# First block of rows ahead of the other rows and the router; search rounds placed behind the scan, with their counts on PE

## The chip, the core and the metric

One Trainium2 chip, and on it one core. The metric is the device time of the kernel in microseconds (us). Five engines with queues of their own work side by side: PE (matrix products; its weight loads are listed as PEld), DVE (vector), ACT (activation functions), POOL (the second vector engine, which also issues indirect transfers) and SP (which issues the other transfers). An instruction waits at the head of its engine's queue until what it needs is done, and all behind it waits too.

## What is computed

Two layers over x, 8 sequences of 256 rows of 128 numbers. Each layer adds an attention-like part and a mixture of experts to its input. The change lies in the first layer alone:

```python
xn = _layernorm(x)
x = x + ssm(xn, ...) + ffn(xn, ...)          # first layer
# ssm: a layer norm of xn, with ln_g and ln_b, then
#   X_main = silu(conv(Xn @ W_up1));  pp = X_main @ W_ll + b_ll
#   delta = softplus(pp[..., :D]);  Bm, Cm = the rest of pp
#   A = -exp(A_log)                           # D = 256 channels, N = 16 states
#   H = exp(delta * A) * H + U;  y = sum_n C * H    (256 steps for each sequence)
#   out = (y * silu(Xn @ W_up2)) @ W_down + b_down
# ffn: scores = softmax(xn @ Wr)              # 2048 rows, 8 experts
#   G, idx = top_k(scores.T, 512)             # each expert takes its 512 best rows
#   out[idx] += G * expert(xn[idx])
```

## The kernel before

**Order of the work.** Inside the first layer the order of PE, ACT, DVE and POOL is the program's own order (`manual_schedule`, L152): what is written first is first in the engine's queue. Generators that `yield` are advanced by hand from the main loop, so the place of a `next(...)` decides where a piece of work stands in every queue.

**Ahead of the scan.** x is loaded in four quarters (L187), then A_log and the weights, all from SP's queue. DVE takes mean and variance of 16 chunks of 128 rows (`bn_stats`, `bn_aggr`, L229 to L234), with A = -exp(A_log) and its reciprocal between them (L231, L232). From these, for all chunks at once, come the scales `rs`, `rv`, `nm` (two square roots on ACT, L235 and L248). POOL builds `dg` (L239: four instructions) and then `wcv`, the weights of W_up1 times the convolution (L242). ACT scales each chunk to `xh` (L279: both layer norms in one), DVE to `xn` (L255); PE transposes both (L272), and ACT and DVE copy the results to `XnT` and `xnT` (L287, L292), quarter by quarter. PE then computes the router's logits `pl` (L736: 16 products with 8 columns), and a softmax follows on DVE and ACT. `xn` and the softmax are written to `xn_d`, from which the experts' rows are gathered.

**`front(q)`** (L303) prepares block q, two sequences of 512 rows: four products `pu` with `wcv` (L314) and a SiLU each (L318), the gate `pg` (L327), delta from `pd` (L353, with softplus by L357 to L375), B and C from `pbc` (L364), and transposes `pxT` (L393), whose halves are swapped by four transfers to `xS` (L402). It yields ten times. Block 0 is prepared ahead of the scan, blocks 1 to 3 inside it (from k = 0, 17 and 33).

**The scan** is a loop over 64 units k (L781; 8 sequences, 4 groups of states, 2 halves of the channels). In each: DVE does `u = (ab - 1) * u` (L688) and the scan (L692); PE does `x_times_b(k + 1)` (u, L670) and `sums(k - 2)` (py, L705); POOL multiplies h by C (L696) and spreads B (L654); ACT computes the decays for k + 2 (L680). u has two PSUM buffers, ab three, h four.

**The search** (L427) finds each expert's threshold, three bits a round, in ten rounds: DVE makes 7 candidates (L429), compares all scores with them (`ge`, L433) and adds up each partition's 16 hits (`cp`, L439); then the generator yields; then PE adds over the partitions (`pc`, L442), and DVE keeps the bits (L447 to L451). Three more pieces find the chosen rows and their slots. Six pieces are advanced by `front(0)`'s yields, the others at the end of the units k = 0 to 7, behind front's piece. The end of the search sets `SEL0` (8 here): from there one expert's rows are selected every 5 units (`select`, L518), and seven units later the experts begin (`experts`, L582; five units each). The rows that they add to, `acc_d`, are first filled with x + xn + bdown by POOL (`base`, L765, one addition in each of the units 0 to 7).

PSUM tiles called `bank(...)` come from one pool with two buffers (`ps_m`), so each waits until the last but one has been read.

Of the kernel before, what the change touches and what calls it, by code (L numbers as in the profile page):

```python
# [8 lines left out]
F32 = mybir.dt.float32  # L9
I32 = mybir.dt.int32  # L10
BF16 = mybir.dt.bfloat16
# [31 lines left out]
SB = 3  # L43
BK = 64
# [6 lines left out]
def block_kernel(ctx: ExitStack, tc: tile.TileContext, a: dict, out: bass.AP):  # L51
# [98 lines left out]
    with ExitStack() as l0:  # L150
# [13 lines left out]

        def exp_and_ln():

            nc.scalar.add_instruction(
                mybir.InstLoadActFuncSet(
                    name=nc.get_next_instruction_name(), act_func_set_id=EXP_LN, ins=[], outs=[]
                )  # L170
            )
# [11 lines left out]

        x = main.tile([P, NC, DM], F32, name="x", tag="c8")
# [3 lines left out]
        alog = load0("alog", [P, ND, N], a["alog"].rearrange("(c p) n -> p c n", p=P))  # L188
# [7 lines left out]
        ln_b = load0("ln_b", [P, 1])  # L196
        wr0 = load0("wr0", [P, E0])
        conv_b = load0("conv_b", [P, ND])
# [6 lines left out]
        wup2 = load0("wup2", [P, D])  # L205
        wll = load0("wll", [P, ND, D + 2 * N], a["wll"].rearrange("(c p) e -> p c e", p=P))
        bll_d = load0("bll_d", [P, ND])
        bll_bc = load0("bll_bc", [2 * N, 1])
# [15 lines left out]
        sd = main.tile([P, NC], F32, name="sd")  # L224
        exp_and_ln()
# [3 lines left out]
        for c in range(NC):  # L229
            if c == 8:  # L230
                nc.vector.tensor_scalar(An, An, -1.0, None, ALU.mult)  # L231
                nc.vector.reciprocal(rA, An)  # L232
            nc.vector.bn_stats(st[:, c, :], x[:, c, :])
            nc.vector.bn_aggr(mv[:, c, :], st[:, c, :])  # L234
        nc.scalar.activation(sd, mv[:, :, 1], AF.Sqrt, bias=eps_t)  # L235

        for dc in range(ND):
            for n in range(0, N, 8):
                nc.gpsimd.tensor_tensor(  # L239
                    dg[:, dc, n : n + 8], bc(eye, 1, 8), bc(rA[:, dc, n : n + 8], 2, BK), ALU.mult  # L240
                )
        nc.gpsimd.tensor_tensor(wcv, bc(wup1, 1, K), conv_w, ALU.mult)  # L242
        rs = main.tile([P, NC], F32, name="rs")
        nc.vector.reciprocal(rs, sd)
        vi = main.tile([P, NC], F32, name="vi")
        nc.vector.tensor_mul(vi, mv[:, :, 1], rs)
        nc.vector.tensor_mul(vi, vi, rs)
        nc.scalar.activation(vi, vi, AF.Sqrt, bias=eps_t)  # L248
        nm = main.tile([P, NC], F32, name="nm")
        nc.vector.scalar_tensor_tensor(nm, mv[:, :, 0], -1.0, rs, ALU.mult, ALU.mult)  # L250
        xn = main.tile([P, NC, DM], F32, name="xn", tag="d8")
        xh = main.tile([P, NC, DM], F32, name="xh", tag="a8")

        def normalize(c):
            nc.vector.tensor_scalar(  # L255
                xn[:, c, :], x[:, c, :], mv[:, c, 0:1], rs[:, c : c + 1], ALU.subtract, ALU.mult
            )

        normalize(0)
        nc.vector.reciprocal(vi, vi)  # L260
        rv = main.tile([P, NC], F32, name="rv")
        nc.vector.tensor_mul(rv, rs, vi)
        nc.vector.tensor_mul(nm, nm, vi)
        xnT = main.tile([P, NT], F32, name="xnT", tag="b8")

        pts = {}

        def transposes(h, lo, src, nm_):
            if lo == 0:
                pts[h, nm_] = ps_u.tile([P, 8, P], F32, name=f"pt_{nm_}{h}", tag="u")  # L270
            for j in range(lo, lo + 4):
                nc.tensor.transpose(pts[h, nm_][:, j, :], src[:, 8 * h + j, :], ident)  # L272

        for h in range(2):
            for g in range(2):
                q = 2 * h + g
                cols = slice(q * BLK, (q + 1) * BLK)
                for c in range(4 * q, 4 * q + 4):
                    nc.scalar.activation(  # L279
                        xh[:, c, :], x[:, c, :], AF.Identity,  # L280
                        bias=nm[:, c : c + 1], scale=rv[:, c : c + 1],
                    )
                    if c:
                        normalize(c)
                transposes(h, 4 * g, xh, "xh")
                transposes(h, 4 * g, xn, "xn")
                nc.scalar.activation(  # L287
                    XnT[:, 2 * q : 2 * q + 2, K - 1 :],
                    pts[h, "xh"][:, 4 * g : 4 * g + 4, :].rearrange("p (b j) l -> p b (j l)", j=2),
                    AF.Identity, bias=ln_b, scale=ln_g,  # L290
                )
                nc.vector.tensor_copy(  # L292
                    xnT[:, cols], pts[h, "xn"][:, 4 * g : 4 * g + 4, :].rearrange("p j l -> p (j l)")
                )
        xn_dv = xn_d.rearrange("(p c) d -> p c d", p=P)
        nc.sync.dma_start(xn_dv[:, :, 0:DM], xn)
# [130 lines left out]
        def search():  # L427
            for i in range(30 // SB):
                nc.vector.tensor_tensor(  # L429
                    cand, bc(thr, 1, NK), bc(bits[:, i, :], 2, E0), ALU.bitwise_or  # L430
                )
                ge = main.tile([P, NK, E0, NC], BF16, name=f"ge{i}", tag="ge")
                nc.vector.tensor_tensor(  # L433
                    ge, bc(sc, 1, NK), bc(cand.bitcast(F32), 3, NC), ALU.is_ge
                )

                cp = main.tile([P, NK, E0], BF16, name=f"cp{i}", tag="cp", bufs=2)
                with nc.allow_low_precision(reason="whole numbers up to 16"):
                    nc.vector.tensor_reduce(cp, ge, AX.X, ALU.add)  # L439
                yield  # L440
                pc = bank(f"pc{i}", [P, NK, E0])
                nc.tensor.matmul(  # L442
                    pc.rearrange("p k e -> p (k e)"), ones_b, cp.rearrange("p k e -> p (k e)"),
                    start=True, stop=True,
                )
                keep = main.tile([P, NK, E0], I32, name=f"keep{i}", tag="keep", bufs=2)
                nc.vector.tensor_scalar(keep, pc, CAP - 0.5, None, ALU.is_ge)  # L447
                m = main.tile([P, E0], I32, name=f"m{i}", tag="m", bufs=2)
                with nc.allow_low_precision(reason="whole numbers up to 7"):
                    nc.vector.tensor_reduce(m, keep.rearrange("p k e -> p e k"), AX.X, ALU.add)  # L450
                nc.vector.scalar_tensor_tensor(  # L451
                    thr, m, 30 - SB * (i + 1), thr, ALU.logical_shift_left, ALU.bitwise_or
                )
# [113 lines left out]
        def scatter(e, s, oc):  # L567
# [6 lines left out]
            if s:  # L574
                tc.declare_no_dep(
                    i.ins, group=f"added{e}", reason="an expert's rows are all different"
                )
            after_all(i, acc0, added[4 * (e - 1) : 4 * e] if e else [])
# [155 lines left out]
        pl = bank("pl", [P, NC, E0])  # L734
        for c in range(NC):
            nc.tensor.matmul(  # L736
                pl[:, c, :], xnT[:, c * P : (c + 1) * P], wr0, start=True, stop=True
            )
        mx = main.tile([P, NC], F32, name="mx")
        nc.vector.tensor_reduce(mx, pl, AX.X, ALU.max)  # L740
        ex = main.tile([P, NC, E0], F32, name="ex")
        nc.vector.tensor_tensor(ex, pl, bc(mx, 2, E0), ALU.subtract)
        exp_and_ln()
        nc.scalar.activation(ex, ex, AF.Exp)
        sm = main.tile([P, NC], F32, name="sm")
        nc.vector.tensor_reduce(sm, ex, AX.X, ALU.add)
        nc.vector.reciprocal(sm, sm)
        nc.vector.tensor_mul(ex, ex, bc(sm, 2, E0))
        nc.sync.dma_start(xn_dv[:, :, DM:], ex)
        nc.vector.tensor_copy(sc, ex.rearrange("p c e -> p e c"))  # L750
        nc.vector.memset(thr, 0)
        find = search()
        next(find)
        for i, _ in enumerate(front(0)):
            if i % 2 and i < 10:
                next(find)
# [6 lines left out]


        def base():  # L765
            for h in range(4):
                t = x[:, 4 * h : 4 * h + 4, :]
                nc.gpsimd.tensor_add(t, t, xn[:, 4 * h : 4 * h + 4, :])
                yield
                nc.gpsimd.tensor_add(t, t, bc(bdown, 1, 4))  # L770
                yield
            acc0.append(nc.sync.dma_start(acc_d.rearrange("(p c) d -> p c d", p=P), x))

        acc0 = []
        running = [find, base()]
        START = {0: [front, 1], 17: [front, 2], 33: [front, 3]}
# [4 lines left out]
        for k in range(len(units) + 4):  # L781
            if k in START:
                f, q = START[k]
                running.insert(0, f(q))
# [5 lines left out]
            part = next(work, None) if 0 in XgT else None  # L790
# [21 lines left out]
            for t in list(running):  # L812
                if next(t, 0) == 0:
                    running.remove(t)
                    if t is find:
                        SEL0 = k + 1
# [609 lines left out]
```

## Time and profile before

| what | us |
|---|---|
| median of 3 runs (lowest, highest) | 701.22 (697.59, 703.15) |
| profiled execution | 702.32 |
| its span, from first to last instruction | 700.4 |
| first transpose on PE | 18.0 |
| first product of block 0 | 35.5 |
| first scan instruction of unit 0 | 68.0 |
| first scan instruction of unit 63 | 431.4 |
| busy: PE, DVE, POOL, ACT | 560.8, 428.2, 381.8, 332.5 |

The profile lists one execution. A line of the timeline has start, duration (both in us), engine, line of the kernel, operation, output and inputs, shapes and the number of instructions merged into it; behind it in brackets the idle time of the engine just before, and what ended that. A line of the stages has the stretch, its length, busy time (and instructions) of PE, PEld, DVE, ACT and POOL, the granted clock of PE, the busy share of the DMA engines and their GB/s.

### The profile page before, as it was taken

The page shows a single profiled execution, that of the slowest core. Times are in us where ns is not written, and L with a number is a line of the kernel's source. Part 1 is how long each engine was busy: PE and PEld are TensorE (multiplying, and loading weights), DVE is VectorE, ACT ScalarE, POOL GpSimd, SP SyncE. Part 2 cuts the span into 40 slices and gives each one's busy share as a digit, 9 for nine tenths or more (in the row PEclk, how much of TensorE's full clock was granted, in tenths as well). Part 3 has the DMA queues.
Part 4 walks back from the last instruction along what each step waited for, and adds up shares of the span by engine and source line. Part 5 has one row for each costly group of instructions (what it writes and reads, how often), then busy time and mean ns, then how long its engine had stood idle before and what let it go on. Part 6 is the DMA issues. An engine that isn't in the chain of part 4 may idle for free.

```text
span 700.4 us, 14519 instructions
## 1 busy us (share of the span) xinstructions
PE 560.8 (80%) x5721; PEld 427.5 (61%) x5721; DVE 428.2 (61%) x669; ACT 332.5 (47%) x763; POOL 381.8 (55%) x320
## 2 busy tenths in 40 slices
PE   0997777789889798989798867497639899999980
PEld 0765545667666776756675756364215498999870
DVE  7367998997647578465666887565117532454333
ACT  2546355556677574677374731243003243555530
POOL 5004646698868789873999896106740022444340
PEclk9997887789989899998898987567558888999995
DMA  7813002222692343321332220122424246888306
GB/s 206 106 24 122 32 31 103 82 78 71 143 181 67 95 108 80 85 60 50 84 96 76 60 80 2 60 91 87 153 84 152 71 128 210 286 276 288 139 27 183
DMA packets 59859, 76.27 MB, mean 109 GB/s; under 512 B 14992, under 2 KB 43808, under 8 KB 59536
## 3 DMA queue, kind: packets, MB, share of 16 engines
q1 hardware_dynamic: 51632, 65.81, 32.6%
q0 software_dynamic: 8160, 9.54, 6.4%
q8 instruction: 45, 0.74, 0.4%
q14 instruction: 22, 0.18, 0.1%
HBM read 59.46 MB, written 13.78 MB: 105 GB/s over the span
## 4 chain that ended last, share of the span: by engine, by line
PE 34%; DVE 10%; issue 9%; POOL 7%; ACT 3%; DMA 2%; SPq 0%; POOLq 0%; DVEq 0%; ACTq 0%
PE ph L1175 6%; PE py L1189 5%; PE py L705 3%; POOL h L696 3%; PE ps L1008 3%; PE u L670 2%; PE pret L1028 2%; DVE u L688 2%; PE ph L603 2%; PE po L621 2%; DVE h L692 2%; POOL acc_d L569 2%; DMA y<-y_d 1%; POOL xg L546 1%; DVE st L1015 1%
## 5 line engine op out<-in xcount | busy, mean ns | idle before, releaser
L696 POOL TENSOR_TENSOR h<-h,Cb 128x1024 f32<-128x1024 f32 x64 | 172.2, 2727 | 32.3 <-DVE h L692 17.4
L692 DVE TENSOR_TENSOR_SCAN h<-ab,u 128x1024 f32<-128x1024 f32 x64 | 146.4, 2287 | 6.3 <-DVE ab L690 0.5
L680 ACT ACTIVATE ab<-delta,An 128x256 f32<-128x256 f32 x256 | 108.5, 498 | 23.2 <-DVE h L692 22.3
L1195 POOL DMA_INDIRECT y_d<-yo,xt x47 | 45.4, 967 | 119.1 <-DVE yo L1194 107.9
L688 DVE SCALAR_TENSOR_TENSOR u<-ab,u 128x1024 f32<-128x1024 f32 x64 | 78.0, 1218 | 48.1 <-PE u L670 33.1
L705 PE MATMUL py<-h,dg 64*64 64x128 f32 x2048 | 81.6, 302 | 23.0 <-POOL h L696 17.3
L670 PE MATMUL u<-Bd,xT 64*128 64x128 f32 x512 | 84.7, 311 | 12.2 <-DVE h L692 11.5
L670 PEld LDWEIGHTS u<-Bd,xT 64*128 64x128 f32 x512 | 71.1, 212 | 29.0 <-issue 14.1
L705 PEld LDWEIGHTS py<-h,dg 64*64 64x64 f32 x2048 | 64.0, 148 | 33.2 <-POOL h L696 21.1
L670 PE MATMUL u<-Bd,xS 64*128 64x128 f32 x512 | 82.3, 312 | 1.2 <-DMA xS<-xT 1.2
L1180 ACT ACTIVATE hid<-ph,wb 128x128 f32<-128x128 f32 x188 | 53.6, 368 | 51.9 <-issue 21.4
L670 PEld LDWEIGHTS u<-Bd,xS 64*128 64x128 f32 x512 | 68.7, 211 | 1.7 <-DMA xS<-xT 1.5
L569 POOL DMA_INDIRECT acc_d<-oc,idx x32 | 51.6, 1611 | 25.5 <-ACT oc L626 19.7
L1015 DVE TENSOR_TENSOR st<-ps,decay_sb 128x384 f32<-128x384 f32 x64 | 31.2, 548 | 52.6 <-remote 29.4
L1175 PE MATMUL ph<-xT,wb 128*128 128x128 f32 x376 | 53.6, 288 | 3.3 <-DVE xT L1169 2.7
L1124 POOL DMA_INDIRECT xs_d<-xk,pos x32 | 32.1, 1002 | 41.9 <-DVE hit L1106 32.5
L1175 PEld LDWEIGHTS ph<-xT,wb 128*128 128x128 f32 x376 | 48.8, 202 | 5.9 <-DVE xT L1169 3.1
L1189 PE MATMUL py<-wb,hid 128*128 128x128 f32 x376 | 51.2, 281 | 0.0
L654 POOL TENSOR_TENSOR Bd<-eye,BT 128x256 f32<-128x256 f32 x64 | 50.5, 992 | 0.0
L1189 PEld LDWEIGHTS py<-wb,hid 128*128 128x128 f32 x376 | 47.3, 198 | 0.0
L621 PEld LDWEIGHTS po<-w,ht 128*128 128x128 f32 x256 | 35.9, 209 | 14.9 <-issue 5.2
L621 PE MATMUL po<-w,ht 128*128 128x128 f32 x256 | 40.5, 303 | 4.5 <-ACT BT L388 2.8
(257 smaller groups left out, 900.9 us busy)
## 6 DMA issues: line engine op xcount, KB each, us to landing
wb<-in_bank_dram SPq DMA_DIRECT2D x47, 514.0 KB
Cb<-C_d SPq DMA_DIRECT2D x32, 512.0 KB
w<-in_w_dram SPq DMA_DIRECT2D x16, 256.0 KB
xs_d<-zrow SPq DMA_DIRECT2D x1, 3031.5 KB
xt<-xs_d SPq DMA_DIRECT2D x11, 260.0 KB
xS<-xT SPq DMA_DIRECT2D x16, 128.0 KB
y<-y_d SPq DMA_DIRECT2D x8, 256.0 KB
decay_sb<-in_decay_dram SPq DMA_DIRECT2D x1, 1536.0 KB
```

Source lines behind the costliest of these rows:

```text
L569: i = nc.gpsimd.indirect_dma_start(out=acc_d, out_offset=bass.IndirectOffsetOnAxis(ap=idx[:, e, s : s + 1], axis=0), in_=oc, in_offset=Non ...
L621: nc.tensor.matmul(po, ht[:, hc, s * P : (s + 1) * P], w2[:, hc, :], start=(hc == 0), stop=(hc == NH - 1),)
L654: nc.gpsimd.tensor_tensor(t[:, w], eye.unsqueeze(1).unsqueeze(1).to_broadcast([P, 2, 2, BK]), bc(BT[b // 2][:, j + 2 * i : j + 2 * i + 2, ...
L670: nc.tensor.matmul(U[k][:, 2 * r : 2 * r + 2, t0 : t0 + BK], xT[b][r ^ half][rows, c, dc * P : (dc + 1) * P], Bd[b, g][rows, 2 * c + half] ...
L680: nc.scalar.activation(ab[k][:, n, :], delta[b // 2][:, dc, (b % 2) * L : (b % 2 + 1) * L], AF.Exp, scale=An[:, dc, g * NG + n : g * NG + ...
L688: nc.vector.scalar_tensor_tensor(U[k], ab[k], -1.0, U[k], ALU.add, ALU.mult)
L692: return nc.vector.tensor_tensor_scan(hf, af, uf, 0.0, ALU.mult, ALU.add)
L696: nc.gpsimd.tensor_mul(hh[k][:, w], hh[k][:, w], Cb[b, g][:, w])
L705: nc.tensor.matmul(pyv[cols, i, dc, :], dg[rows, dc, g * NG + n, :], hh[k][rows, n, j * P : (j + 1) * P], start=(g == 0 and dc == 0 and n ...
L1175: nc.tensor.matmul(ph[:, hc, :], w[:, hc * P : (hc + 1) * P], xTs[t], start=True, stop=True)
L1180: nc.scalar.activation(hids[t][:, hc, :], ph[:, hc, :], AF.Relu, bias=w[:, DI + NH * DM + hc : DI + NH * DM + hc + 1],)
L1189: nc.tensor.matmul(py, hids[t][:, hc, :], w[:, DI + hc * DM : DI + (hc + 1) * DM], start=(hc == 0), stop=(hc == NH - 1),)
```

## The change

- A_log is loaded ahead of x, and its exponential is the first work of ACT; the negation and the reciprocal follow the statistics. `wcv` is put ahead of `dg` in POOL's queue. conv_b, wll, bll and wup2 are loaded ahead of wr0 and bits.
- 24 products of the identity with itself stand first in PE's queue.
- Scales are computed for chunks 0 to 3 first, then for 4 to 15. Only block 0's chunks are scaled, transposed and copied (two halves) ahead of `front(0)`.
- The rest is a generator, `others()`: three turns with one quarter of the other rows each, then the last quarter's `xn`, the router's logits with the softmax, then the search. The copies to `xnT` move from DVE to ACT. Of its pieces, eight are advanced by `front(0)`'s yields (1 to 9 without 7), and one in each unit from k = 0 on, right behind the scan and ahead of `x_times_b(k + 1)`. By this count the search ends in unit 10 (`SEL0` = 10).
- In a round, the addition `cp` on DVE is left out; PE does 16 products that add up in PSUM, one for each chunk, with columns 16 elements apart.
- `base()` starts when the search has ended, with two additions in a unit.

```diff
+WARM = 24
...
+        alog = load0("alog", [P, ND, N], a["alog"].rearrange("(c p) n -> p c n", p=P))
         x = main.tile([P, NC, DM], F32, name="x", tag="c8")
...
-        alog = load0("alog", [P, ND, N], a["alog"].rearrange("(c p) n -> p c n", p=P))
...
+        nc.gpsimd.tensor_tensor(wcv, bc(wup1, 1, K), conv_w, ALU.mult)
+
+        def variance(c):
             nc.vector.bn_stats(st[:, c, :], x[:, c, :])
             nc.vector.bn_aggr(mv[:, c, :], st[:, c, :])
...
+        def deviations(cs):
+            nc.scalar.activation(sd[:, cs], mv[:, cs, 1], AF.Sqrt, bias=eps_t)
+            nc.vector.reciprocal(rs[:, cs], sd[:, cs])
...
+        def inner(c):
+            nc.scalar.activation(
+                xh[:, c, :], x[:, c, :], AF.Identity, bias=nm[:, c : c + 1], scale=rv[:, c : c + 1]
+            )
+
+        def inner_rows(c0, n, name):
+
+            pt = bank(f"pt_xh{name}", [P, n, P])
+            for j in range(n):
+                nc.tensor.transpose(pt[:, j, :], xh[:, c0 + j, :], ident)
+            nc.scalar.activation(
+                XnT[:, c0 // 2 : (c0 + n) // 2, K - 1 :],
+                pt.rearrange("p (b j) l -> p b (j l)", j=2),
+                AF.Identity, bias=ln_b, scale=ln_g,
+            )
...
+        def outer_rows(q):
+            pt = bank(f"pt_xn{q}", [P, 4, P])
+            for j in range(4):
+                nc.tensor.transpose(pt[:, j, :], xn[:, 4 * q + j, :], ident)
+            nc.scalar.copy(xnT[:, q * BLK : (q + 1) * BLK], pt.rearrange("p j l -> p (j l)"))
+
+
+        warm = bank("warm", [P, P])
+        for _ in range(WARM):
+            nc.tensor.matmul(warm, ident, ident, start=True, stop=True)
+        for c in range(4):
+            variance(c)
+        deviations(slice(0, 4))
+        for c in range(4, NC):
+            variance(c)
+        for c in range(2):
+            inner(c)
+        inner_rows(0, 2, "0a")
+        for c in range(2, 4):
+            inner(c)
+        deviations(slice(4, NC))
+        inner_rows(2, 2, "0b")
...
-                cp = main.tile([P, NK, E0], BF16, name=f"cp{i}", tag="cp", bufs=2)
-                with nc.allow_low_precision(reason="whole numbers up to 16"):
-                    nc.vector.tensor_reduce(cp, ge, AX.X, ALU.add)
                 yield
                 pc = bank(f"pc{i}", [P, NK, E0])
-                nc.tensor.matmul(
-                    pc.rearrange("p k e -> p (k e)"), ones_b, cp.rearrange("p k e -> p (k e)"),
-                    start=True, stop=True,
-                )
+                for c in range(NC):
+                    nc.tensor.matmul(
+                        pc.rearrange("p k e -> p (k e)"), ones_b,
+                        ge[:, :, :, c].rearrange("p k e -> p (k e)"),
+                        start=(c == 0), stop=(c == NC - 1),
+                    )
...
+        def others():
+            for q in range(1, 4):
+                for c in range(4 * q, 4 * q + 4):
+                    inner(c)
+                inner_rows(4 * q, 4, str(q))
+                outer(q - 1)
+                outer_rows(q - 1)
+                yield
+            outer(3)
+            outer_rows(3)
+            nc.sync.dma_start(xn_dv[:, :, 0:DM], xn)
+            yield
+            pl = bank("pl", [P, NC, E0])
...
+            nc.scalar.activation(ex, ex, AF.Exp)
+            yield
...
+            yield from search()
...
+        find = others()
+        ahead = front(0)
+        for i, _ in enumerate(ahead):
+            if i >= 1 and i != 7:
                 next(find)
...
-        running = [find, base()]
+        running = []
...
+            if SEL0 is None and next(find, 0) == 0:
+                SEL0 = k
+                running.append(base())
```

## Prediction

> **What bounds the kernel now.** I read the page first, then the busy time by stage, then each engine's timeline through the first 155 us. Only the work ahead of the scan over 64 units (0 to 66.6 us) and the scan's first 15 units are touched; from 442 us on (second layer) nothing changes. The stages, with columns of busy time for PE, PEld, DVE, ACT and POOL, then the granted clock, DMA share and GB/s:
>
> ```profile
> 18.00:28.60 10.60, 9.40 (x31) 5.83 (x32) 5.25 (x16) 8.33 (x19) 0.00 (x0) 1.00 0.97 55
> 28.60:35.50 6.90, 6.90 (x35) 6.90 (x34) 0.69 (x1) 1.68 (x2) 0.00 (x0) 1.00 0.64 161
> 35.50:66.60 31.10, 25.56 (x128) 17.39 (x130) 22.00 (x43) 17.07 (x29) 7.21 (x8) 0.87 0.24 60
> 66.60:122.00 55.40, 42.05 (x406) 30.45 (x406) 51.66 (x71) 26.26 (x52) 33.18 (x24) 0.80 0.17 62
> 122.00:154.80 32.80, 26.34 (x427) 22.03 (x426) 30.71 (x34) 16.50 (x46) 24.87 (x18) 0.79 0.26 77
> 154.80:405.00 250.20, 222.40 (x2727) 166.00 (x2725) 166.05 (x160) 161.03 (x340) 203.66 (x150) 0.92 0.40 91
> 405.00:433.70 28.70, 21.63 (x404) 18.38 (x404) 25.39 (x23) 8.85 (x22) 22.14 (x13) 0.82 0.12 39
> ```
>
> To 18 us PE is idle; then it transposes all rows, then does the router's logits, and only then the first block. From 66.6 to 154.8 us DVE bounds (93% busy), from 154.8 to 405 us PE (89%), and in the last units DVE again, at 3.65 us a unit.
>
> How fast PE runs decides the first stage. The timeline of PE there:
>
> ```profile
> 28.83 6.83 PE L736 MATMUL pl<-wr_sb,xnT 128*128 128x8 f32 x32
> 35.52 6.63 PE L314 MATMUL pu<-XnT,wcv 128*128 128x256 f32 x16
> 42.71 3.73 PE L314 MATMUL pu<-XnT,wcv 128*128 128x256 f32 x16 [0.54 <-ACT xm L318]
> ```
>
> The same 16 products take 6.63 us, then 3.73. Single steps are 427 ns up to 41.2 us and 216 after: the clock was half until PE had done 5.9 us of 256-column products on end. Neither the transposes from 18 us nor the logits (steps of 213 ns, like every 128-column load at half clock) raised it. The page's clock row says 1.0 there; the durations decide.
>
> ACT by turns, one quarter (four chunks scaled, then their transposes copied out after 0.57 us):
>
> ```profile
> 20.26 1.64 ACT L279 ACTIVATE xh<-x,nm,rv 128x128 f32<-128x128 f32 x4
> 22.46 0.78 ACT L287 ACTIVATE XnT<-pt_xh,ln_b_sb,ln_g_sb 128x512 f32<-128x512 f32 x1 [0.57 <-PE pt_xh L272]
> ```
>
> DVE in one unit with a round of the search:
>
> ```profile
> 73.62 1.22 DVE L688 SCALAR_TENSOR_TENSOR u<-ab,u 128x1024 f32<-128x1024 f32 x1
> 75.01 2.29 DVE L692 TENSOR_TENSOR_SCAN h<-ab,u 128x1024 f32<-128x1024 f32 x1
> 77.21 0.19 DVE L447 TENSOR_SCALAR keep<-pc 128x56 int32<-128x56 f32 x1
> 77.44 0.25 DVE L450 TENSOR_REDUCE m<-keep 128x8 int32<-128x56 int32 x1
> 77.72 0.17 DVE L451 SCALAR_TENSOR_TENSOR py<-m,py 128x8 int32<-128x8 int32 x1
> 77.93 0.22 DVE L429 TENSOR_TENSOR py<-py,bits 128x56 int32<-128x56 int32 x1
> 78.19 1.09 DVE L433 TENSOR_TENSOR ge<-sc,py 128x896 bf16<-128x896 f32 x1
> 79.31 1.09 DVE L439 TENSOR_REDUCE cp<-ge 128x56 bf16<-128x896 bf16 x1
> ```
>
> No gap between them: 6.7 us a unit (unit starts 66.59, 73.62, 80.31, 87.05, 93.74).
>
> **The change, part by part. 1. The start.** The first product needs `wcv` (POOL):
>
> ```profile
> 9.79 4.08 POOL L239 TENSOR_TENSOR dg<-eye,rA 128x512 f32<-128x512 f32 x4 [6.67 <-DVE eye L83]
> 13.83 2.34 POOL L242 TENSOR_TENSOR wcv<-wup_sb,conv_w 128x1024 f32<-128x1024 f32 x1
> ```
>
> Now `wcv` comes ahead of `dg`. The 4 KB packets of `conv_w` ran from 6.0 to 8.5 us, so it starts near 9.1 and ends at 11.4. `alog` first in SP's queue costs x one issue, 0.5 us: statistics of the first four chunks 4.2 to 5.8, five constants 0.8, `rs` and `vi` 0.35, and the rest up to the scaling 1.14 (as from 16.23 to 17.37 before): 8.1; chunks 0 and 1 are copied out by 10. So the first product moves from 35.52 to 11.4: -24.1. The exponential, the warming products (idle PE) and `dg` (needed two units into the scan) cost nothing under this cover.
>
> What comes back, in order:
> - The second half of the first block waits in ACT's queue behind the square roots for chunks 4 to 15; DVE reaches these after twelve times 0.39 us, at 12.8. Copied out at 14.5, SiLU table loaded at 15.8, second SiLU done at 17 to 18.7. From the first product 5.6 to 7.3, before 7.1 (35.52 to 42.66): -0.6.
> - Two turns with other rows, each on a ring of ACT and PE with two PSUM banks: 1.64 scaling, 1.35 until the quarter is copied out and the bank is free, 8 product steps (3.42 at half clock, 1.72 at full), 0.65 for wait and SiLU: 7.1 to 7.25 or 5.5. Before, the same two SiLUs took 4.3 (42.66 to 46.95). I take 13.6 for both: +9.3.
> - Third turn and the gates: 1.64 + 5.6 = 7.2, before 2.4: +4.8.
> - Last quarter's transposes, its copy on ACT (0.6) and the table load before delta: +2.
> - The logits now stand between delta's two products on PE, and ACT's exponential of the router stands ahead of delta's second half: 6.83 by the row, with what is warm or cold around: +7 (3.4 to 8). In the old place they were paid too; that is inside the -24.1.
> - DVE is free when `z` comes, where it was 1.5 us late (ACT done at 56.54, DVE began at 58.10): -1.5.
> - Between `z` and the first unit's start lie two rounds, in DVE's and PE's order ahead of `delta + w` and of u: count (2.1), 2.0 on DVE, `delta` 1.2, ab 1.65, count, 2.0 again: 12.3 where it was 8.5: +3.8.
>
> Sum: -24.1 - 0.6 + 9.3 + 4.8 + 2 + 7 - 1.5 + 3.8 = **+0.7**: the first scan starts where it did. With every product at full clock it is -11, with all at half clock and counts of 2.5, +4.6.
>
> Here a rule speaks. The Trainium skill (TensorE: Matmul & The Clock Gate, Parts 1 and 4) says that some 3.4 us of sustained work raise the clock, one such window of idleness drops it, and a transpose does not count as work. Rule and rows agree on transposes. If the 24 warming products held through the turns, the sum would be -11; but they end near 10 us and the turns leave PE 3.4 us of counted work in 7.2. The trace dropped the clock after a like stretch (1.3 us of products in the 3.4 before 75.6), so I take the rows.
>
> **2. The search.** Per unit DVE now has 3.65 + 2.1 = 5.75 us, 1.0 less. But three rounds instead of six are begun ahead of the scan, and the search ends at unit 10 instead of 7. Before, 15 units to the first expert: 122.04 - 66.59 = 55.45 for 0 to 7, and 32.7 for 8 to 14 (4.06 each plus `z`, `delta` 2.4 and one selection's 1.85): 88.2. After, 17 units: 7 x 5.75 = 40.3; units 7 to 9, 6.85 + 7.7 + 3.9 (before 7.65, 9.24, 3.84; PE's counts no longer stand behind `pd`, and POOL's base additions no longer hold up 1.17 us subtractions) + 2.4; unit 10 with its selection 7.57 + 1.85; six at 4.06 = 24.4: 95.0. The two units come off the tail, where one costs 3.65: -7.3. Net 95.0 - 88.2 - 7.3 = **-0.5**.
>
> **3. The counts on PE.** 16 loads and products of 56 columns instead of one. No row has them; the nearest:
>
> ```profile
> 131.72 0.61 PE L533 MATMUL pi<-rr,ol 128*32 128x32 bf16 x16
> ```
>
> 32-column loads, contiguous data: 0.6 us is the low end. Four times the load and 56 columns make 1.2 at full clock, 2.1 at half. The skill's SBUF — State Buffer (The DMA port swizzle, on cachelines) says that accesses each falling on another 16-byte line slow down; here neighbours lie 32 bytes apart, so 2.4 or more. In a unit with `pu`, PE has 0.95 (u) + 1.0 (py) + 1.75 (pu) + count against DVE's 5.75: room for 2.05. By the row it is hidden; by the rule 0.35 too long in four units, +1.4. I take +0.5; ends 0 and +12 (rival C). Behind the count u and py are queued on PE, and DVE's next unit waits for u.
>
> **4. The base rows.** Eight additions of 1.27 us moved from units 0 to 7, where POOL had 33 us in 55, to units 10 to 13, two a unit: 10.2 us beside the multiplications by C and the gathers. POOL is then 8 us late at unit 15; h has four buffers and PE takes a unit's product two units later, so most is absorbed. +1.5 (0 to +6). The `acc_d` write still precedes the first scatter by four units.
>
> Sum: 0.7 - 0.5 + 0.5 + 1.5 = **+2.2**. The profiled execution took 702.32 (span 700.4 and 1.9 around it), the median is 701.22: 704.5 for that one, 703.4 against the median.
>
> **Rivals.**
> - A, as summed: 703.4, own range 696 to 709. For it: PE and ACT in a ring at half clock. Against: the clock in five stretches is worked out, not seen.
> - B, faster: the clock is high through turns, gates and logits; -11 in place of +0.7: 692. For it: warming products and denser PE. Against: the rows above.
> - C, slower: the count with its strided reads is over 2.05 us at full clock. Then PE, not DVE, sets units 0 to 6; at half clock count, u, py, pu are 2.1 + 1.7 + 2.0 + 3.4 = 9.2 against 5.75, and where half of the seven units run so it is 3.5 x 3.45 = +12 in place of +0.5: 715. Against: a PE that never pauses got the full clock at 41.4.
> - D, POOL's lateness reaches the gathers that the first expert's transposes wait for: +6 in place of +1.5: 708.
>
> **How the numbers follow.** A 0.48, B 0.20, C 0.20, D 0.12. Faster by over 1% (about what a measurement can tell) is below 694.2: B and a little of A, 0.22. Slower is above 708.2: C, half of D, some of A, 0.32. Rest 0.46. The range leaves out one in ten at each end: 692 to 714.
>
> **What would show it.** First product near 11.5 and first scan near 67 us: step 1 right; at 58 or less, B. Steps of `pu` in the turns 427 ns: half clock. Units 0 to 6 apart by 5.75: DVE bounds; 7 or more with DVE waiting on `pc` or u: C. POOL's multiplication more than 8 us behind its scan at unit 15, and PE waiting for `xg`: D. A shift anywhere after 442 us would make the whole account wrong.

## The result, and the profile after

| | before | after |
|---|---|---|
| median of 4 runs (lowest, highest), us | 700.47 (697.59, 703.15) | 709.65 (704.99, 714.70) |
| ratio, 95% interval | | 1.0144 (1.0099, 1.0188) |
| profiled execution, its span, us | 702.32, 700.4 | 707.55, 705.6 |
| first unit begins (DVE's `u`) | 66.59 | 58.82 |
| first unit with an expert begins | 154.78 (unit 15) | 170.43 (unit 17) |
| unit 63 begins | 429.93 | 436.76 |

The kernel became 1.4% slower: about 9 us by the medians, 5.2 in the two profiled spans. Ratios and intervals, here and below, leave out slow executions (over 1.5% above the fastest of the same kernel); the profiled ones of the experiments e4, e14 and e18 were such, so nothing behind unit 17 is read from them. The scan ends 6.8 us later; what follows it is 1.6 us shorter, without any edit there. In the scan a line number of after is 12 to 15 above that of before (`u` on DVE L702, scan L706, `py` L719, `h` L710, `ge` L448, `pc` L454).

The stages of after, cut at the same events as those shown of before (columns as there):

```profile
0.00:58.80 58.80, 46.06 (x260) 32.62 (x260) 25.59 (x91) 32.57 (x61) 14.64 (x32) 0.88 0.58 118
58.80:143.20 84.40, 67.08 (x719) 53.88 (x719) 66.62 (x99) 35.75 (x73) 39.93 (x26) 0.82 0.16 52
143.20:170.40 27.20, 18.36 (x314) 15.78 (x311) 22.76 (x23) 9.36 (x26) 22.19 (x18) 0.81 0.24 89
```

The start is 7.8 us shorter. But in the stage with the search DVE is busy for 66.6 of 84.4 us (79%), where it was at 93%. DVE has less to do and waits more; the question is for what.

First the start, PE's timeline of after:

```profile
12.03 2.00 PE L329 MATMUL pu<-XnT,wcv 128*128 128x256 f32 x8 [0.38 <-POOL wcv L240]
...
19.65 2.00 PE L329 MATMUL pu<-XnT,wcv 128*128 128x256 f32 x8 [0.43 <-ACT XnT L269]
...
24.94 2.00 PE L329 MATMUL pu<-XnT,wcv 128*128 128x256 f32 x8 [0.43 <-ACT XnT L269]
...
30.24 3.44 PE L342 MATMUL pg<-XnT,wup_sb 128*64 128x256 f32 x16 [0.43 <-ACT XnT L269]
...
36.19 3.63 PE L762 MATMUL pl<-wr_sb,xnT 128*128 128x8 f32 x32
```

Eight products of `pu` take 2.00 us in both turns: full clock, where the forecast had 3.42. A turn takes 5.3 us (19.65 to 24.94) instead of 7.1 to 7.25, and the logits 3.63 instead of 6.8. The gates (3.44) and the second product of `pd` (3.62, the first 1.98) were at half clock.

Then the unit in which the spacing breaks. Units 0 to 2 are 5.57 us long, then 9.61, 8.45, 7.01, 6.95, 7.58, 8.00, 7.79 and, in unit 10, 12.32. DVE at the end of unit 2 and in unit 3:

```profile
74.53 1.09 DVE L448 TENSOR_TENSOR ge<-sc,py 128x896 bf16<-128x896 f32 x1
75.54 1.22 DVE L702 SCALAR_TENSOR_TENSOR u<-ab,u 128x1024 f32<-128x1024 f32 x1
...
76.93 2.29 DVE L706 TENSOR_TENSOR_SCAN h<-ab,u 128x1024 f32<-128x1024 f32 x1
83.14 0.22 DVE L460 TENSOR_SCALAR keep<-pc 128x56 int32<-128x56 f32 x1 [3.93 <-PE pc L454]
...
83.68 0.17 DVE L464 SCALAR_TENSOR_TENSOR py<-m,py 128x8 int32<-128x8 int32 x1
...
84.14 1.09 DVE L448 TENSOR_TENSOR ge<-sc,py 128x896 bf16<-128x896 f32 x1
85.15 1.22 DVE L702 SCALAR_TENSOR_TENSOR u<-ab,u 128x1024 f32<-128x1024 f32 x1
```

And PE over the same time (its lines for u are left out):

```profile
75.77 1.99 PE L719 MATMUL py<-h,dg 64*64 64x128 f32 x32 [2.73 <-DVE ge L448]
77.68 3.78 PE L329 MATMUL pu<-XnT,wcv 128*128 128x256 f32 x8
81.26 1.85 PE L454 MATMUL pc<-ge,ones_b 128*128 128x56 bf16 x16
...
85.38 1.99 PE L719 MATMUL py<-h,dg 64*64 64x128 f32 x32 [1.18 <-DVE ge L448]
```

DVE waits 3.93 us for the count. The comparison that this count adds up (`ge`, at 74.53, in unit 2) was done at 75.6; the count stands behind `py` and `pu`, and `py`, which reads only h and dg, waited for that very `ge`. It can't be for data. The search keeps its thresholds and candidates (`thr`, `cand`, later `jl`, `jh`, `tok`) in the unused half of the PSUM tile `py`: the operand `py` in DVE's line of `ge` is that table. The PSUM page of the Trainium skill (PSUM — Partial Sum Buffer, on bank collisions) says that two engines may not touch one PSUM bank, at the same partitions, at once, and that software has to order them by bank, not by address. In this trace DVE's accesses to the table and PE's writes of the sums take turns in the program's order; no run here shows what would happen without that, nor whether the waits follow the bank or the whole tile. With the search piece now ahead of `sums(k - 2)`, that order closes a ring, once a unit: `ge` of unit k, then `py` (1.0 to 2.0), then front's product (2.0 to 3.8), then the count of unit k + 1 (1.8), then DVE's `keep` to `ge` (2.1). At full clock that is 6.9, at half 9.7: the spacing measured, 7.0 and 9.6 (unit 4, at 8.45, changes clock halfway). Units 0 and 1 have no `py` product yet; in unit 2, whose `py` is the first, the wait only begins.

The same coupling twice more, DVE's selection and the `py` products in front of it:

```profile
141.53 0.69 DVE L533 TENSOR_TENSOR ol<-iota_f,py 128x512 bf16<-128x512 f32 x1 [2.19 <-PE py L719]
...
165.04 0.69 DVE L533 TENSOR_TENSOR ol<-iota_f,py 128x512 bf16<-128x512 f32 x1 [3.12 <-PE py L719]
```

```profile
139.48 1.99 PE L719 MATMUL py<-h,dg 64*64 64x128 f32 x32 [7.56 <-DVE py L528]
...
163.21 1.62 PE L719 MATMUL py<-h,dg 64*64 64x128 f32 x32 [3.63 <-POOL h L710]
```

In unit 10 PE stands 7.56 us until DVE has written the slots (`jl`, `jh`, `tok`) into the same banks, and then DVE waits for PE. In unit 15 POOL is late with h (it has the base rows), so `py` is late, so DVE's `ol`, which reads a table in that bank, waits 3.12 us, and with it the next unit.

### The profile page after: what moved, and what is told of

It reads as the page before. It is cut to its first block, busy times and chain, and to the rows that moved or that the text cites. A ratio compares the mean times of both kernels' runs of the same rounds, so it can differ in the third digit from the quotient of the medians.

```text
span 705.6 us, 14924 instructions
## 1 busy us (share of the span) xinstructions
PE 570.8 (81%) x5919; PEld 436.7 (62%) x5919; DVE 417.8 (59%) x662; ACT 333.4 (47%) x769; POOL 382.5 (54%) x320
## 5 line engine op out<-in xcount | busy, mean ns | idle before, releaser
L710 POOL TENSOR_TENSOR h<-h,Cb 128x1024 f32<-128x1024 f32 x64 | 173.4, 2745 | 49.0 <-DVE h L706 36.7
L706 DVE TENSOR_TENSOR_SCAN h<-ab,u 128x1024 f32<-128x1024 f32 x64 | 146.3, 2286 | 5.9
L719 PE MATMUL py<-h,dg 64*64 64x128 f32 x2048 | 79.9, 300 | 34.7 <-POOL h L710 19.6
L702 DVE SCALAR_TENSOR_TENSOR u<-ab,u 128x1024 f32<-128x1024 f32 x64 | 78.0, 1219 | 50.3 <-PE u L684 36.7
L719 PEld LDWEIGHTS py<-h,dg 64*64 64x64 f32 x2048 | 62.9, 147 | 44.4 <-POOL h L710 25.0
L1209 ACT ACTIVATE hid<-ph,wb 128x128 f32<-128x128 f32 x188 | 53.5, 368 | 49.2 <-ACT hid L1209 20.1
L1204 PE MATMUL ph<-xT,wb 128*128 128x128 f32 x376 | 53.1, 287 | 3.0 <-DVE xT L1198 2.7
L1218 PE MATMUL py<-wb,hid 128*128 128x128 f32 x376 | 49.8, 276 | 0.0
L635 PEld LDWEIGHTS po<-w,ht 128*128 128x128 f32 x256 | 34.4, 203 | 16.4 <-issue 5.2
L635 PE MATMUL po<-w,ht 128*128 128x128 f32 x256 | 38.9, 297 | 5.8 <-ACT gate L351 2.4
```

The costliest lines, as they stand in the source:

```text
L635: nc.tensor.matmul(po, ht[:, hc, s * P : (s + 1) * P], w2[:, hc, :], start=(hc == 0), stop=(hc == NH - 1),)
L702: nc.vector.scalar_tensor_tensor(U[k], ab[k], -1.0, U[k], ALU.add, ALU.mult)
L706: return nc.vector.tensor_tensor_scan(hf, af, uf, 0.0, ALU.mult, ALU.add)
L710: nc.gpsimd.tensor_mul(hh[k][:, w], hh[k][:, w], Cb[b, g][:, w])
L719: nc.tensor.matmul(pyv[cols, i, dc, :], dg[rows, dc, g * NG + n, :], hh[k][rows, n, j * P : (j + 1) * P], start=(g == 0 and dc == 0 and n ...
L1204: nc.tensor.matmul(ph[:, hc, :], w[:, hc * P : (hc + 1) * P], xTs[t], start=True, stop=True)
```

## The experiments

Theory T: the search's tables share PSUM banks with `py`, and the place of the search ahead of `py` turns this into a ring. Rivals: C of the prediction (u, `py`, front's products and 16 counts are simply too long for PE), P (the base rows are what costs), and for the start W (the warming products made the clock).

The experiments ran in three groups, the first (e1, e2, e3, e7) on another chip than the second (e4, e5, e8, e14) and the third; the kernel before took 698.05, 664.13 and 662.40 us there (43 runs each). So kernels are compared by their ratio to the kernel before of their own group, and by the length of stages. Stages vary too: in two profiles of the changed kernel, units 3 to 9 differ by 2.3 us, and 33 of the 39 us between the two lie behind the start of unit 63. In the table the columns behind the interval are when unit 0 begins, the lengths of units 0 to 2, 3 to 9, 10, and 11 to 16, and when unit 17, the first with an expert, begins, all in the profiled execution.

| kernel | ratio | 95% interval | start | 0-2 | 3-9 | 10 | 11-16 | unit 17 |
|---|---|---|---|---|---|---|---|---|
| forecast for after | 1.003 | | 67.3 | 17.3 | 43.9 | 9.4 | 24.4 | 162.2 |
| after | 1.0144 | 1.0099-1.0188 | 58.82 | 16.7 | 55.4 | 12.3 | 27.2 | 170.43 |
| after, group 3 | 1.0122 | 1.0077-1.0167 | 59.69 | 16.7 | 53.1 | 12.1 | 27.4 | 169.01 |
| e1 search behind sums | 1.0022 | 0.9998-1.0047 | 58.51 | 16.7 | 49.2 | 10.0 | 28.0 | 162.35 |
| e2 tables in SBUF | 1.0370 | 1.0299-1.0441 | 60.31 | 23.0 | 56.4 | 10.6 | 26.2 | 176.41 |
| e3 cp on DVE | 1.0130 | 1.0063-1.0197 | 61.55 | 20.1 | 48.8 | 12.5 | 28.0 | 170.83 |
| e4 no warming | 1.0161 | 1.0112-1.0210 | 59.71 | 16.7 | 55.5 | 12.3 | 27.4 | 171.56 |
| e5 base rows as before | 1.0073 | 1.0044-1.0101 | 60.28 | 16.7 | 58.3 | 11.0 | 23.5 | 169.79 |
| e8 = e1 + e5 | 0.9894 | 0.9852-0.9936 | 59.22 | 17.4 | 48.0 | 8.9 | 23.5 | 156.99 |
| e14 contiguous counts | 1.0079 | 1.0048-1.0111 | 61.12 | 18.5 | 50.4 | 12.1 | 27.0 | 169.06 |
| e18 = e8 + contiguous, from ex | 0.9849 | 0.9791-0.9907 | 60.34 | 16.7 | 45.3 | 8.9 | 23.5 | 154.75 |
| e19 the start alone | 0.9997 | 0.9966-1.0027 | 61.49 | 20.4 | 50.9 | 8.9 | 23.5 | 165.16 |
| e20 = e8 with cp | 0.9993 | 0.9967-1.0019 | 60.85 | 20.1 | 49.8 | 8.9 | 23.5 | 163.09 |

**e1: the search behind the sums.**

```diff
-            if SEL0 is None and next(find, 0) == 0:
-                SEL0 = k
-                running.append(base())
...
                 sums(k - 2)
+            if SEL0 is None and next(find, 0) == 0:
+                SEL0 = k
+                running.append(base())
```

> The changed kernel, with the search piece of a unit moved from ahead of x_times_b(k + 1) to behind sums(k - 2); nothing else. Theory T (py's products wait for the compare ge of the same unit, because the search's tables thr, cand, jl, jh stand in the tile py that these products write; with the counts behind them this closes a ring of 7.0 us at full and 9.6 at half clock): units 3 to 9, now 9.6, 8.5, 7.0, 7.0, 7.6, 8.0, 7.8 apart, come down to 5.6 to 6.5; the end of unit 9 comes 8 to 11 us earlier, and the whole 7 to 11 us: 699 to 702. Rival C of the prediction (u, py, pu and 16 counts are simply too long for PE at a low clock): the same products stand in the ring of PE, so units stay at 7 to 9 and the time at 709. Rival P (POOL's base rows are what costs): unchanged up to unit 9, time within 2 us of 709.

Measured: 1.0022, and units 3 to 9 at 6.78, 5.64, 5.71, 8.27, 7.01, 7.02, 8.75; unit 17 begins 8.1 us earlier (6.7 against the changed kernel's second profile), and unit 10 6.5, where 8 to 11 was expected. PE's timeline in unit 4 of e1:

```profile
82.73 1.10 PE L719 MATMUL py<-h,dg 64*64 64x128 f32 x32
83.77 1.81 PE L454 MATMUL pc<-ge,ones_b 128*128 128x56 bf16 x16
85.51 1.95 PE L342 MATMUL pg<-XnT,wup_sb 128*64 128x256 f32 x16
```

At full clock `py`, a count as long as before and front's product follow each other without a wait, and the unit takes 5.64 us; in the changed kernel units at full clock took 7.0. So C falls as the account of the whole loss: the count isn't too long where it stands behind `py`. What remains of C are units 3 and 6 (6.78 and 8.27), where a product of front at half clock stands ahead of the count (`pu` 3.53, `pd` 3.09) and DVE waits 1.1 and 2.5 us for it.

**e2: the tables in SBUF.**

```diff
-        tab = py[:, 0, L:]
+        tab = main.tile([P, L], F32, name="tab")
...
-        tab1 = py[:, 1, L:]
+        tab1 = main.tile([P, L], F32, name="tab1")
```

> The changed kernel with the search's tables (thr, cand, jl, jh, tok) in SBUF tiles of their own instead of in the free half of the PSUM tile py; order of the program unchanged. Theory T: no product py waits for DVE in the search any more (7.5 us in units 3 to 7 and 7.6 in unit 10 before), units 3 to 9 at 5.6 to 6.5, and unit 10 falls from 12.3 to some 8: 10 to 14 us earlier at unit 16, whole 696 to 700, better than moving the piece behind the sums by 2 to 4 us, since unit 10's wait goes too. Rival C: no change, 709. If DVE's reads of SBUF tables make POOL slower (both are in use at once), units get longer by 0.3 to 1 us and part of the gain is lost.

The waits were as T says: between 58 and 145 us no `py` product waits for DVE any more, where it had been 7.5 us behind `ge` and 7.6 behind the slots. The time was not: 3.7% slower than before. All units with a round take 7.4 to 8.4 us. DVE in units 0 and 1 of e2, and POOL at the same time:

```profile
64.42 2.02 DVE L464 SCALAR_TENSOR_TENSOR tab<-m,tab 128x8 int32<-128x8 int32 x1
...
71.84 2.02 DVE L464 SCALAR_TENSOR_TENSOR tab<-m,tab 128x8 int32<-128x8 int32 x1
```

```profile
64.08 2.34 POOL L710 TENSOR_TENSOR h<-h,Cb 128x1024 f32<-128x1024 f32 x1 [8.96 <-DVE h L706]
71.49 2.35 POOL L710 TENSOR_TENSOR h<-h,Cb 128x1024 f32<-128x1024 f32 x1 [5.08 <-DVE h L706]
```

An update of eight numbers takes 2.02 us instead of 0.17, and ends within 0.02 us of POOL's multiplication (66.44 and 66.42, 73.86 and 73.84). The SBUF page of the Trainium skill (SBUF — State Buffer, two separate sides) has it: a DVE instruction with two inputs in SBUF and a POOL instruction that reads SBUF exclude each other. With the tables in PSUM one input isn't in SBUF; that they share `py`'s banks is the price. The selections, which read these tables, suffer in the same way: an `ol` that begins 0.2 us behind a POOL multiplication (198.93 and 198.75) takes 3.34 us instead of 0.69. So e2 confirms the wait, but its time says nothing for or against T. A PSUM bank of their own for the tables was not tried.

**e3: cp back on DVE.** The diff shown with the change, undone for `cp` and the 16 products.

> The changed kernel with the addition cp back on DVE and one count product of contiguous columns instead of 16 strided ones; place of the search unchanged. Theory T: the ring through py's wait stays, shorter by the count's 1.7 us: 5.3 us at full and 7.9 at half clock; DVE needs 5.6 + 1.1 = 6.7. So units 0 to 2 get longer (6.7 instead of 5.6) and units 3 to 9 lie at 6.7 to 8, in sum 2 to 6 us shorter; the two rounds ahead of unit 0 each lose the 1.7 of the count and gain 1.1: whole 703 to 708. Rival C (the counts alone cost): units 3 to 9 at 6.7, as in the kernel before, whole 700 to 703.

As T expects: units 0 to 2 at 6.7, units 3 to 9 at 6.5 to 7.7 (the ring without the count's 1.7), unit 10 still 12.5, the start 2.7 us later; 1.013. C's 700 to 703 isn't met. Units 3 to 9 alone (48.8 in sum) would nearly fit C's 6.7 each; against it stand the total and unit 10.

**e7: the kernel before, with the search right behind the scan, and nothing else.**

```diff
-        running = [find, base()]
+        running = [base()]
...
+            if SEL0 is None and next(find, 0) == 0:
+                SEL0 = k
             part = next(work, None) if 0 in XgT else None
...
-                    if t is find:
-                        SEL0 = k + 1
```

> The kernel before, with one part of the change alone: in a unit the search piece stands right behind the scan and ahead of x_times_b(k + 1), with cp on DVE; start, base rows and the six pieces ahead of the scan as before. Theory T: py's products now wait for ge of the same unit in this kernel too; the ring is 5.3 us at full and 7.9 at half clock against DVE's 6.7, so that units 2 to 7 get 0 to 1.2 us longer, and the unit in which the slots are written 2 to 5 more: whole +2 to +8, 703 to 709. If the place does nothing by itself (rival C: the counts alone cost): 699 to 702.

A miss in the total, 0.9972 (0.9946 to 0.9998), with the stages as expected: units 0 to 8 take 66.3 instead of 61.9 us, unit 7, where the slots are written, 11.3 instead of 7.6 (1.9 of that is a wait for `py`, 1.9 the first selection, which stood in unit 8). The place alone thus costs 4.4 us in this kernel too. What I had overlooked is that the search's end is now seen one unit earlier, so that the first expert begins in unit 14, at 154.71 us, where it was unit 15 at 154.78: the loss is made up there, and one unit of the scan moves from ahead of the experts to behind them. In spite of that unit, unit 63 begins 2.7 us earlier; the experts' products `po` run from 159.6 to 391.5 us, where it was 159.7 to 395.6. Why they take 4 us less is open.

**e4: no warming products** (`WARM = 0`).

> The changed kernel without the 24 warming products (WARM = 0). Theory W (these products raised the clock, and the turns then kept it, which is why the scan starts at 58.8 us and not near 67): pu's steps in the first product and in the turns are 427 ns again, a turn takes 7.1 instead of 5.3 us, and the first unit starts at 63 to 67 us; whole 713 to 718. Rival (the dense products of the turns themselves raise the clock): only the first pu is at 427 ns, first unit at 59 to 61, whole 709 to 711.

W falls as far as the time goes. PE's timeline of e4:

```profile
12.35 6.43 PE L329 MATMUL pu<-XnT,wcv 128*128 128x256 f32 x16 [0.23 <-POOL wcv L240]
...
22.08 2.00 PE L329 MATMUL pu<-XnT,wcv 128*128 128x256 f32 x8 [0.43 <-ACT XnT L269]
```

Only the first 16 products are at half clock; behind them the turns run at full clock without any warming. The first unit begins at 59.71 instead of 58.82, and the ratio of 1.0161 can't be told from 1.0144. Nor did warming secure the clock elsewhere: all twelve profiles with this start have the first turn at 2.00 us, but the second was at or near half clock in six (e3, e5, e14, e18, e19, e20), as here in e5:

```profile
19.68 2.00 PE L329 MATMUL pu<-XnT,wcv 128*128 128x256 f32 x8 [0.43 <-ACT XnT L269]
...
24.97 3.56 PE L329 MATMUL pu<-XnT,wcv 128*128 128x256 f32 x8 [0.43 <-ACT XnT L269]
```

**e5: the base rows in units 0 to 7, and e8: e5 and e1 together.**

```diff
-                running.append(base())
...
-        running = []
+        running = [base()]
```

> The changed kernel with the base rows placed as before: one POOL addition in each of the units 0 to 7 instead of two in each of units 10 to 13; nothing else. Step 4 of the prediction (moving them costs 1.5 us, 0 to 6): unit 10, now 12.3 us long, and unit 15 get shorter by 2 to 5 us together, units 0 to 7 stay within 0.3 us, whole 705 to 708. Theory T (the ring through py's wait carries the loss): units 3 to 9 stay at 7.0 to 9.6 us.

> The changed kernel with two edits: the search piece behind sums(k - 2), as in the first experiment, and the base rows in units 0 to 7. If the two losses are separate, the second comes off the first experiment's 698.8: units 9, 10 and 15, there 8.75, 9.98 and 9.58 us, lose 2 to 6 us together, since POOL is no longer between two of DVE's instructions that want the same memory: 693 to 697, below both kernels. If POOL's additions in units 0 to 7 delay h and with it py, units 4 to 7 grow and the time stays at 698 to 701.

In e5 unit 10 is 1.3 us shorter and units 11 to 16 3.7, unit 15 alone going from 8.57 to 5.34; the ring stays (units 3 to 9 at 7.0 to 9.6). In e8 the ring is gone as in e1, and units 10 and 11 to 16 are 1.1 and 4.4 us shorter than there: 0.9894. That is 2.3 to 2.5% better than the changed kernel, no less than e1 (1.0 to 1.2%) and e5 (0.5 to 0.7%) together. So the two losses are separate, and e8 beats both kernels.

**e14 and e18: the counts on contiguous columns.** `ge` is laid out chunk by chunk; in e18, on top of e8, the comparison reads the softmax's own tile `ex` instead of `sc`.

```diff
-                ge = main.tile([P, NK, E0, NC], BF16, name=f"ge{i}", tag="ge")
+                ge = main.tile([P, NC, NK, E0], BF16, name=f"ge{i}", tag="ge")
...
-                    ge, bc(sc, 1, NK), bc(cand.bitcast(F32), 3, NC), ALU.is_ge
+                    ge, bc(ex, 2, NK), bc(cand.bitcast(F32), 1, NC), ALU.is_ge
...
-                        ge[:, :, :, c].rearrange("p k e -> p (k e)"),
+                        ge[:, c, :, :].rearrange("p k e -> p (k e)"),
```

> The changed kernel with ge laid out chunk by chunk, so that each of the 16 count products reads 56 contiguous columns; place and number of products unchanged. Step 3 of the prediction had two prices for them, 1.2 us at full and 2.1 at half clock by the row of contiguous columns, 2.4 by the rule on strided lines; measured are 1.8 at both clocks. If the stride sets the 104 ns a step, the count falls to 1.1 to 1.3 at full clock and follows the clock; the ring loses 0.5 us in units 3 to 6, whole 707 to 709. If not, 104 ns stay. In either case theory T leaves units 3 to 9 at 7 to 9 us. DVE's comparison, which now reads the scores with a stride, may take longer than 1.09 us; each 0.1 is 1 us in all.

> The same version (search behind sums, base rows in units 0 to 7) with the 16 count products on contiguous columns, and DVE's comparison reading the scores in the softmax's own order (ex), contiguous too. The count takes 0.6 us at full and 0.9 at half clock instead of 1.8; ge stays at 1.09 us if its strided read was what made it 1.68. DVE bounds units 0 to 5 at 5.6 already, so the gain is in units 2 and 6 (6.2 and 8.3 us) and in the two counts ahead of unit 0: 3 to 5 us, 0.982 to 0.987 of the kernel before. If ge takes 1.68 in this order too: 0.99 to 0.993.

PE's lines of e14 at half and at full clock:

```profile
73.58 0.88 PE L455 MATMUL pc<-ge,ones_b 128*128 128x56 bf16 x16 [2.56 <-DVE ge L448]
...
84.62 0.57 PE L455 MATMUL pc<-ge,ones_b 128*128 128x56 bf16 x16
```

The stride did set the price: 0.6 and 0.9 us instead of 1.8, which had been the same at both clocks (1.1 to 1.3 was expected at full clock). In e14 the comparison pays for it (1.68 us instead of 1.09, since it reads `sc` across its rows). In e18 it stays at 1.09: units 0 to 6 all take 5.57 to 5.64 us, DVE without a gap, and the time is 0.9849 of before, the best seen, though its interval overlaps e8's.

**e19 and e20: the start alone, and e8 without the counts on PE.** e19 has the search at the unit's end, cp on DVE, and the base rows in units 0 to 7; e20 is e8 with cp on DVE.

> The changed kernel with everything but the new start taken back: search at the unit's end behind front's piece, cp on DVE with one count product, base rows in units 0 to 7. The start alone then remains, with three rounds instead of six ahead of the scan. Step 1 of the prediction with the clock as it turned out (full in the turns): first unit at 60 to 62 us instead of 66.6, 5 to 6 us gained; of step 2 the other side: three rounds more inside the scan at 3.1 us each against two units of 3.65 off the tail, +9 us less 1 for a selection that begins one unit earlier. Whole +2 to +5 us, 1.003 to 1.008 of the kernel before. If the rounds are hidden where they now stand, the ratio is 0.99 to 1.00.

> The version with the search behind sums(k - 2) and the base rows in units 0 to 7 (0.989 of the kernel before), with cp on DVE and one contiguous count product. This takes out step 3 alone: each of the ten units costs DVE 1.09 us more, the first unit starts 2.5 us later (as with cp in the changed kernel), and PE is 1.7 us shorter where it sets a unit (units 2 and 6): +8 to +11 us, 1.000 to 1.006. If the 16 products cost what they save: 0.987 to 0.991.

e19 comes out even (0.9997, where 1.003 to 1.008 was the main expectation): the first unit begins 5.1 us earlier, and the three rounds that are now inside the scan take most of that back, so that unit 63 begins 1.2 us earlier. e20 against e8 gives step 3 alone: 0.9993 against 0.9894, about 1% that the counts on PE gain, once they no longer stand in the ring.

**The changed kernel once more**, for the third group's chip.

> The changed kernel once more, unchanged, so that it stands on the same chip as the three others of this group (the last group's chip was 5% faster as a whole, so that groups are compared by their ratio to the kernel before). Every theory: 1.010 to 1.019 of the kernel before.

1.0122. There PE was at full clock again from unit 4 on, and units 4 to 6 took 6.96, 7.01 and 6.95 us: the ring of 7.0. In unit 3 (8.59) `py` and `pu` still ran in part at half clock (1.64 and 3.10).

## Why the prediction came out as it did

The time lies in the range, but by luck: the forecast +2.2 was two errors of opposite sign, 8.5 us too much for the start and 14.6 too little for the units. Measured to the start of unit 63: -7.8 (start) + 23.4 (111.6 us for units 0 to 16, against 88.2 for 0 to 14) - 8.8 (the units behind) = +6.8. The forecast had +0.7 + 8.8 - 7.3 = +2.2.

- **Step 1, wrong by 8.5 us, most of it the clock.** The turns ran at full clock, as rival B had it, though without its -11, and e4 has it without the warming products. By my estimate from the trace, 5.4 of the 8.5 came with the clock: the second SiLU ended at 16.9 us (17.9 in the sum), the two turns took 10.6 (13.6), and the logits added 5.6 to the stretch up to `w` (7). Another 1.3 was a slip in adding: the terms listed for the last stretch give 11.05 and not 12.3, and 10.98 was measured (47.84 to 58.82). The rest is small terms. I weighed the skill's rule of the clock gate (TensorE: Matmul & The Clock Gate, Part 1) against a row of this kernel and took the row, "1.3 us of products in the 3.4 before". But the rule speaks of a window of idleness of some 3.4 us, and at full clock the pause between the `pu` groups of two turns is 3.3 us (21.65 to 24.94). I had worked with turns at half clock, 7.2 long, and so took the case for granted that I was to decide. That does not make the rule a forecast: at this pause six of the twelve profiles lost the full clock before the second turn, and six did not. Of the parts, the first product at 12.03 was right (11.4).
- **Step 2, right where DVE alone counts, wrong in the order.** Units 0 to 2 took 5.57 (5.75). What failed is the assumption that the search has no tie to `py`: I listed what is queued behind the count (u and `py`), but not what `py` itself waits for when DVE's table lies in its banks. That is 55.4 us for units 3 to 9 instead of 43.9, and in unit 10 12.3 instead of 9.4. e1 gives back 8.5 us of units 3 to 10 (6.0 against the second profile of the changed kernel). With the order, the base rows and the counts mended (e18), the scan takes 45.3, 8.9 and 23.5 us, 3% above the forecast's 43.9, and 6% and 4% below its 9.4 and 24.4.
- **Step 3.** The count took 1.8 us: 1.2 to 2.1 was forecast by the row of contiguous columns, 2.4 by the rule on cachelines. The room of 2.05 held in e1 and e8. The rule was right that the stride sets the price (0.6 to 0.9 without it) and wrong by a third in its size as I estimated it; the page names no size.
- **Step 4, +1.5 forecast, 0 to 6 as its ends; measured 5.0 to 5.5** (units 10 to 16 of e5 against after, and of e8 against e1). Four buffers of h did not absorb the lateness, since `ol` on DVE waits for the latest `py`.
- **Rival C** was to show itself by "7 or more with DVE waiting on pc", and just that was seen, with a time between D's 708 and C's 715. Its mechanism wasn't the main one: e1 keeps the counts and loses most of the wait. The sign did not tell a long count from a count that is queued behind something held up. **D** was right that POOL's lateness matters, but its way led through `py` to DVE, not through `xg`.

## What to carry to other kernels

A table in the free half of a PSUM tile ties the engine that uses it to the one that writes the tile, and then each must be placed behind the other's last use, not only behind its data. When a piece is moved in one engine's order, ask of everything that it overtakes what that waits for, by bank as well as by value. And a wait for X shows where X stands in its queue, not that X is long: look first at what X's own queue waited for.

## What the runs showed of the hardware

- A 16-bit moving operand with neighbours 32 bytes apart: 16 products of 56 columns took 1.82 us at both clocks; contiguous, 0.58 at full and 0.9 at half clock.
- DVE's comparison of 896 elements, float input read along the row or across it: 1.09 against 1.68 us.
- Behind a group of 2.0 us of products at full clock and a pause of 3.3 us with transposes in it, the next products ran at full clock 11 times of 18 in the twelve profiles with this start (second turn 6 of 12; gates behind a second turn at full clock 5 of 6). So 3.3 us is at the edge here.
- DVE with two inputs in SBUF beside a POOL multiplication that began first (e2): 2.02 us instead of 0.17 for eight numbers.
